# Two placeholder activations around the group norm, in a four-layer vision network

## The chip, the cores and the metric

The kernel runs on one core of one Trainium2 chip. Its time is the device time of one execution in microseconds (us), and of several runs the median counts.

## The reference

The input is four images of 56 by 56 pixels with 128 channels. Each image passes through four layers, and each layer adds its result to its input. Every layer begins with a group norm over groups of four channels:

- L0 and L3 are window transformers. Windows of 7 by 7 pixels (shifted by 3) attend within themselves with four heads; then the whole image of 3136 pixels attends to itself with four heads, after a layer norm; then comes a two-layer network with a Gelu, after another layer norm.
- L1 is a state-space layer: a projection, a 3 by 3 convolution of each channel with a Silu, a softplus for the step sizes, a scan over the image in four directions with 16 states, a layer norm, a gate and a projection back.
- L2 is a deformable convolution: offsets from a 3 by 3 convolution, a gather of four neighbours for each of nine taps, their weighted sum and a product with the kernel.

The part that matters here, as the kernel computes it: for each group of four channels, the mean and the variance over channels and pixels, then (x - mean) / sqrt(variance + 1e-5).

## The kernel before, in words

All data is kept as channels by pixels: 128 partitions, 3136 columns, worked on in 7 chunks of 448. `run` loops over the images; for each it calls `swin("L0")`, `mamba`, `deform` and `swin("L3")` on the same tile `x`. Inside each layer the order of instructions on each engine is the order in which they are written (`manual_schedule`).

- Statistics (`stats`, line 115) are taken by VectorE chunk by chunk, as soon as the layer before has stored a chunk. `group_norm` (line 117) joins them: VectorE aggregates (line 121), TensorE averages the means over each group with a matrix (line 123), VectorE makes the group variances (lines 125 to 128), TensorE averages those (line 130, tile `gn_pv`), ScalarE takes the root (line 132), VectorE the reciprocal (line 133). Three calls lead to it: in `attention` (both transformers), in `mamba_conv` and in `deform`.
- In a transformer, `windows` (line 197) returns the steps of the window attention, and the loop in `attention` writes them out interleaved: tokens (line 222, VectorE and GpSimd, the normalised pixels `xw`), project (line 230, TensorE, `pq` and `pk`), queries and keys (lines 235 and 241, ScalarE, Identity with a bias), scores (lines 257 to 264), exponentials (line 267, ScalarE, Exp), and so on. GpSimd fills several tiles with zeros at the start (lines 219, 225, 323, 324, 377). The layer norm of the image attention follows the windows and takes a root for each chunk (line 158), so that Exp and Sqrt alternate from the fourth row of windows on.
- The last step of a transformer, `mlp`, ends on ScalarE with the Gelu (line 680) and on VectorE with the store of a chunk (line 690). After L3 the chunk is written out and the next image's chunk is read into the same columns (`finish`, lines 1381 and 1383).
- `mamba_conv` starts with the normalised chunks (line 137), the projection (line 765, tile `pi`), its copies by ScalarE (line 769) and the convolution; its first function with a table of its own is Silu (line 791).
- `deform` uses only copies and Identity on ScalarE after its group norm.

ScalarE works from a table of functions that has to be loaded when the next function is not in the one at hand. No line of the kernel asks for it: the compiler puts an ACT_TABLE_LOAD ahead of the first activation that needs another table, and the profile books it under that activation's line. Copy, Identity and Square need none.

Of the kernel before, what the change touches and what calls it, by code (L numbers as in the profile page):

```python
# [10 lines left out]
F32 = mybir.dt.float32  # L11
F32R = mybir.dt.float32r
I32 = mybir.dt.int32
AF = mybir.ActivationFunctionType
# [5 lines left out]
P = 128  # L20
# [50 lines left out]
def _offsets(cols):  # L71
    at, n = {}, 0
    for name, w in cols:
        at[name] = (n, w)
        n += w
    return at, n


class _Net:
    def __init__(self, ctx, tc, x, packs, out):  # L80
        self.tc, self.nc, self.x_in, self.out = tc, tc.nc, x, out
        self.B = x.shape[0]
        nc = self.nc
        wp = ctx.enter_context(tc.tile_pool(name="weights", bufs=1))
        self.keep = wp
        self.w = {}
        for i, (layer, cols) in enumerate(COLS.items()):
            at, n = _offsets(cols)
            t = wp.tile([P, n], F32, tag=f"w_{layer}", name=f"w_{layer}")
            (nc.sync if i % 2 == 0 else nc.scalar).dma_start(t, packs[layer])  # L90
            self.w[layer] = {name: t[:, o : o + k] for name, (o, k) in at.items()}
        c = self.w["C"]
        self.ident, self.gmat = c["ident"], c["gmat"]
        self.ones = {1: c["ones1"], 2: c["ones2"]}
        self.center = {1: (c["center1"],), 2: (c["center2"], c["others2"])}
        self.sel = wp.tile([P, KB], F32R, tag="sel", name="sel")
        nc.vector.memset(self.sel.bitcast(F32), 0.0)
        for h in range(NH):
            nc.vector.memset(self.sel[h * DK : h * DK + 2, :].bitcast(F32), 1.0)
        self.ident2 = wp.tile([64 + NX, NX], F32R, tag="ident2", name="ident2")  # L100
        nc.vector.memset(self.ident2.bitcast(F32), 0.0)
        for k in (0, 64):
            nc.vector.tensor_copy(self.ident2[k : k + NX, :], self.ident[:NX, :NX])
        self.one32 = wp.tile([P, DK], F32, tag="one32", name="one32")
        nc.vector.memset(self.one32, 1.0)
        self.eps = wp.tile([P, 1], F32, tag="eps", name="eps")
        nc.vector.memset(self.eps, 1e-5)
        self.x = wp.tile([P, L], F32, tag="x", name="x")
        self.st = wp.tile([P, NCK, 6], F32, tag="gn_st", name="gn_st")
        self.dpool = ctx.enter_context(tc.tile_pool(name="tables", bufs=1, space=DRAM))  # L110


    def stats(self, x, c):

        self.nc.vector.bn_stats(self.st[:, c, :], x[:, c * CH : (c + 1) * CH])

    def group_norm(self, sb, ps):
        nc = self.nc
        st = self.st
        mv = sb.tile([P, 2], F32, tag="gn_mv", name="gn_mv")  # L120
        nc.vector.bn_aggr(mv, st.rearrange("p c s -> p (c s)"))
        pm = ps.tile([P, 512], F32, tag="mm", name="gn_pm")
        nc.tensor.matmul(pm[:, 0:1], lhsT=self.gmat, rhs=mv[:, 0:1], start=True, stop=True)
        mean = sb.tile([P, 1], F32, tag="gn_mean", name="gn_mean")
        nc.vector.tensor_copy(mean, pm[:, 0:1])
        dv = sb.tile([P, 1], F32, tag="gn_dv", name="gn_dv")
        nc.vector.tensor_sub(dv, mv[:, 0:1], mean)
        nc.vector.scalar_tensor_tensor(dv, dv, dv, mv[:, 1:2], ALU.mult, ALU.add)
        pv = ps.tile([P, 512], F32, tag="mm", name="gn_pv")
        nc.tensor.matmul(pv[:, 0:1], lhsT=self.gmat, rhs=dv, start=True, stop=True)  # L130
        rstd = sb.tile([P, 1], F32, tag="gn_rstd", name="gn_rstd")
        nc.scalar.activation(rstd, pv[:, 0:1], AF.Sqrt, bias=self.eps)
        nc.vector.reciprocal(rstd, rstd)
        return mean, rstd
# [172 lines left out]
    def attention(self, layer, x, x1, oT, sb):  # L307
# [32 lines left out]
        with tc.manual_schedule():  # L340
# [33 lines left out]
            with tc.tile_pool(name="ap_sb", bufs=2) as tb, tc.tile_pool(name="ap_ps", bufs=8, space=PSUM) as ps:  # L374
                bank = lambda name: ps.tile([P, 512], F32, tag="mm", name=name)
                of_windows = self.windows(layer, x, x1, self.group_norm(tb, ps), tb, bank)
                nc.gpsimd.memset(kl, 0.0)
                ln = {}

# [1108 lines left out]
```

## Time and profile before

| what | value |
|---|---|
| median of 3 runs | 13458.64 us (13451.59 to 13462.05) |
| profiled execution, its own time | 13245.72 us |
| its span from first to last instruction | 13243.9 us |
| mean granted TensorE clock | 0.933 |
| ScalarE busy | 7563.6 us (57%) |
| ACT_TABLE_LOADs under line 132 | 8, of 1283 ns each |
| ACT_TABLE_LOADs under line 267 | 48, of 1283 ns each |
| group norms (line 132, ACTIVATE) | 16, of 261 ns each |

By the first instruction of each group norm, one image takes some 860 us in L0, 1220 us in L1, 367 us in L2 and 862 us in L3. Engines in the profile are PE (TensorE), PEld (its weight loads), DVE (VectorE), ACT (ScalarE), POOL (GpSimd) and SP (SyncE, which issues most DMAs). A line of the timeline gives the start, the duration, the engine, the line of the kernel, the operation, its output and inputs; in brackets stands the idle time of the engine ahead of it and what ended that. A line of the stretches gives the busy time and the number of instructions of PE, PEld, DVE, ACT and POOL in order, then the granted clock, the busy share of the DMA engines and GB/s.

### The profile page before, as it was taken

The numbers are of one execution on the slowest core, as the hardware profiler recorded it, in microseconds if no ns is written. First come the engines' busy times: TensorE is split into PE (matmuls) and PEld (weight loads), VectorE is DVE, ScalarE is ACT, GpSimd is POOL, SyncE is SP. The second block draws the span as 40 slices with busy tenths as digits, with TensorE's granted clock in tenths as the row PEclk, the third lists the DMA queues.
The fourth block names the chain that finished last, engine by engine and source line by source line (L and its number), as shares of the span: only waits on it lengthen the run. The fifth ranks groups of instructions, "written<-read, shape, count | busy, mean of one in ns | idle before, by whom it ended". The sixth has DMA issues, their size and how long they took to land. (4 is left out here: it accounts for less than half of the span.)

```text
span 13243.9 us, 218251 instructions
## 1 busy us (share of the span) xinstructions
PE 11713.7 (88%) x85716; PEld 7459.5 (56%) x85716; DVE 9575.5 (72%) x11831; ACT 7563.6 (57%) x19130; POOL 9941.6 (75%) x6852
## 2 busy tenths in 40 slices
PE   8999995699898999579989899957999989995799
PEld 4448884444544888444454488834445448883444
DVE  6649996665665999666466499966646649996664
ACT  5567772356556777235655677723565567772356
POOL 4949995488494999548849499954975949995497
PEclk9999997799999999779999999977999999996799
DMA  2000004200000000420000000042000000004200
GB/s 100 1 14 4 5 4 118 78 1 6 6 1 14 4 5 4 120 75 1 8 4 1 14 5 5 4 125 70 1 9 2 1 14 5 5 4 130 65 1 6
DMA packets 181178, 344.60 MB, mean 26 GB/s; under 512 B 20104, under 2 KB 101416, under 8 KB 180024
## 3 DMA queue, kind: packets, MB, share of 16 engines
q0 software_dynamic: 80640, 231.28, 6.3%
q1 hardware_dynamic: 99224, 97.83, 2.4%
q8 instruction: 678, 11.11, 0.4%
q14 instruction: 348, 2.85, 0.1%
q10 hardware_dynamic: 288, 1.53, 0.0%
HBM read 256.04 MB, written 74.52 MB: 25 GB/s over the span
## 5 line engine op out<-in xcount | busy, mean ns | idle before, releaser
L555 POOL TENSOR_TENSOR es<-es,e 128x896 f32<-128x896 f32 x2016 | 4158.8, 2088 | 133.0 <-ACT e L549 75.0
L350 DVE TENSOR_REDUCE mx<-pm 128x1 f32<-128x512 f32 (+1 forms) x4928 | 3056.5, 670 | 1411.1 <-PE pm L349 795.8
L549 ACT ACTIVATE e<-pst 128x448 f32<-128x448 f32 (+1 forms) x5600 | 2677.6, 544 | 1893.3 <-PE pst L547 1348.1
L1066 DVE TENSOR_TENSOR_SCAN hs<-da,dbu 128x928 f32<-128x928 f32 x1792 | 3633.0, 2070 | 53.2 <-ACT dbu L1059 29.3
L1075 POOL TENSOR_TENSOR hs<-hs,cb 128x896 f32<-128x896 f32 x1792 | 3486.9, 1963 | 26.0 <-ACT carry L1070 20.8
L349 PE MATMUL pm<-ks,qs 32*128 32x512 f32 (+1 forms) x9856 | 2911.8, 636 | 13.4 <-DVE nm L371 7.8
L547 PE MATMUL pst<-qs,ks 32*128 32x448 f32 x11200 | 2685.4, 547 | 0.0
L1084 PE MATMUL yt<-w_C,hs 128*116 128x128 f32 x14336 | 1865.8, 273 | 1.1 <-POOL hs L1075 1.1
L542 PE MATMUL pst<-nm,sel 32*128 32x448 f32 x5600 | 1638.7, 614 | 0.0
L1084 PEld LDWEIGHTS yt<-w_C,hs 128*116 128x116 f32 x14336 | 1570.5, 135 | 2.1 <-POOL hs L1075 2.1
L1048 PE MATMUL dbu<-dgb,ut 112*128 112x224 f32 x7168 | 1258.5, 298 | 268.8 <-DVE hs L1066 268.7
L571 PE MATMUL po<-e,va 128*32 128x448 f32 (+1 forms) x11200 | 1352.4, 551 | 0.1
L349 PEld LDWEIGHTS pm<-ks,qs 32*128 32x128 f32 x9856 | 924.3, 186 | 745.2 <-DVE mx L350 618.9
L1325 POOL DMA_INDIRECT g<-tab,idx x1008 | 940.5, 933 | 452.9 <-issue 425.8
L1048 PEld LDWEIGHTS dbu<-dgb,ut 112*128 112x128 f32 x7168 | 945.3, 192 | 534.2 <-DVE hs L1066 524.2
L1002 ACT ACTIVATE da<-dl,A 128x112 f32<-128x112 f32 x3584 | 1194.6, 383 | 0.1
L547 PEld LDWEIGHTS pst<-qs,ks 32*128 32x128 f32 x11200 | 1098.0, 185 | 102.6 <-issue 13.7
L1351 PE MATMUL pvt<-w_C,g 112*128 112x112 f32 x2016 | 404.5, 367 | 729.3 <-issue 607.8
L542 PEld LDWEIGHTS pst<-nm,sel 32*128 32x128 f32 x5600 | 570.6, 184 | 740.2 <-DVE mx L350 387.1
L1352 ACT COPY vt<-pvt 128x336 f32<-128x336 f32 x336 | 147.2, 438 | 1188.0 <-PE pvt L1351 1184.5
L1351 PEld LDWEIGHTS pvt<-w_C,g 112*128 112x128 f32 x2016 | 315.2, 203 | 823.1 <-issue 784.2
L1070 ACT COPY carry<-hs 128x32 f32<-128x32 f32 x1792 | 397.5, 222 | 623.3 <-DVE hs L1066 615.2
(230 smaller groups left out, 15791.4 us busy)
## 6 DMA issues: line engine op xcount, KB each, us to landing
tab<-zero SPq DMA_DIRECT2D x4, 6728.0 KB
g<-tab,idx POOLq DMA_INDIRECT x1008, 3.5
tab<-gt SPq DMA_DIRECT2D x32, 448.0 KB
dl_d<-dl SPq DMA_DIRECT2D x28, 448.0 KB
dl<-dl_d SPq DMA_DIRECT2D x56, 224.0 KB
tab<-gt SPq DMA_DIRECT2D x32, 336.0 KB
out_dram<-x SPq DMA_DIRECT2D x28, 224.0 KB
x<-in_x_dram SPq DMA_DIRECT2D x21, 224.0 KB
```

The lines of the kernel that those rows point to most:

```text
L349: nc.tensor.matmul(pm[:, :m], lhsT=qs[head(h), q.start : q.start + P], rhs=ks[head(h), keys], start=True, stop=True)
L350: nc.vector.tensor_reduce(mx[:, home[i][1], h, kc : kc + 1], pm[:, :m], AX.X, ALU.max)
L542: nc.tensor.matmul(t[:, :CH], lhsT=self.sel[head(h), :], rhs=nm[head(h), part(qc)], start=True, stop=False)
L547: nc.tensor.matmul(t[:, :CH], lhsT=ks[head(h), k * KB : (k + 1) * KB], rhs=qs[head(h), part(qc)], start=False, stop=True)
L549: nc.scalar.activation(e[:nk, j, :], t[:nk, :CH], AF.Exp, scale=SCALE)
L555: nc.gpsimd.tensor_tensor(s, es[g - 1, p][:nk] if k == 1 else s, e[:nk], ALU.add)
L571: nc.tensor.matmul(m["po"][head(h), :CH], lhsT=va[:nk, k, head(h)], rhs=src(h)[:nk], start=(k == 0), stop=(k == NKB - 1))
L1002: nc.scalar.activation(m["da"][:, :, n, 2:], dl(), AF.Exp, scale=A[:, j, n : n + 1])
L1048: nc.tensor.matmul(pu[:, 8 * h : 8 * h + 8, 2 + tb * TB : 2 + (tb + 1) * TB], lhsT=made[g]["ut", 2 * r + tb][:, d, :], rhs=made["r", g // ...
L1066: nc.vector.tensor_tensor_scan(flat(pairs[u // 2][:, d % 2]), flat(made[g]["da"][:, r]), flat(banks.pop(u)), 0.0, ALU.mult, ALU.add)
L1075: nc.gpsimd.tensor_tensor(hs, hs, made["r", g // 2]["cb"][:, :, r * HW : (r + 1) * HW], ALU.mult)
L1084: nc.tensor.matmul(sums[q][:YR, e * P : (e + 1) * P], lhsT=hs[:, n, :], rhs=self.ident, start=(n == 0), stop=(n == NST // 2 - 1), is_trans ...
```

## The change

A helper `table_of(f)` writes one activation of function `f`, 128 by 1, from the constant tile `eps` into a new tile `any` that nothing reads. `group_norm` calls it with Sqrt as its first instruction, ahead of the aggregation, in all four layers. `attention` calls it with Exp straight after its group norm, ahead of the first instruction of the windows. Nothing else is moved or removed; which table is loaded where follows from the compiler.

```diff
+        self.any = wp.tile([P, 1], F32, tag="any", name="any")
...
+    def table_of(self, f):
+
+        self.nc.scalar.activation(self.any, self.eps, f)
+
     def group_norm(self, sb, ps):
         nc = self.nc
         st = self.st
+        self.table_of(AF.Sqrt)
         mv = sb.tile([P, 2], F32, tag="gn_mv", name="gn_mv")
...
                 of_windows = self.windows(layer, x, x1, self.group_norm(tb, ps), tb, bank)
+                self.table_of(AF.Exp)
                 nc.gpsimd.memset(kl, 0.0)
```

## The prediction

> **What bounds the kernel now.** I read the page's busy times first, then the stretches by stage, then ScalarE's groups by line, and last the timeline around the group norms.
>
> ```profile
> PE 11713.7 (88%) x85716; PEld 7459.5 (56%) x85716; DVE 9575.5 (72%) x11831; ACT 7563.6 (57%) x19130; POOL 9941.6 (75%) x6852
> ```
>
> ScalarE (ACT) is busy 57% of the span, so a change to it counts only where another engine stands still for it. In the stretches, TensorE is busy over 90% in every transformer and scan stage, and half busy in the four gather stages. All those stages begin with a group norm, and there nothing runs beside the chain. The groups of ScalarE by line (columns: count, busy us, mean ns, idle before) show the table loads:
>
> ```profile
> L158 ACT ACT_TABLE_LOAD x132 | 169.4, 1283 | 2.3
> L132 ACT ACT_TABLE_LOAD x8 | 10.3, 1283 | 56.2 <-PE gn_pv L130 56.2
> L267 ACT ACT_TABLE_LOAD x48 | 61.6, 1283 | 0.8
> L132 ACT ACTIVATE gn_rstd<-gn_pv,eps 128x1 f32<-128x1 f32 x16 | 4.2, 261 | 99.3 <-PE gn_pv L130 99.2
> ```
>
> There are 16 group norms (4 images by 4 layers) and 8 loads. The view of line 132 gives the wait for gn_pv in front of a load 7 times, in front of the ACTIVATE 9 times. So 7 loads begin only when the variance is there. The timeline of one of them, the second image's first layer (start us, duration):
>
> ```profile
> 3326.12 2.89 ACT L680 ACTIVATE h<-ph,w_L 128x448 f32<-128x448 f32 x4 [1.11 <-PE ph L679]
> ...
> 3338.56 1.80 POOL L225 MEMSET pz<- 128x2048 f32 x1
> ...
> 3339.81 1.28 ACT L132 ACT_TABLE_LOAD   x1 [10.80 <-PE gn_pv L130]
> 3341.10 0.26 ACT L132 ACTIVATE gn_rstd<-gn_pv,eps 128x1 f32<-128x1 f32 x1
> 3341.39 0.16 DVE L133 RECIPROCAL gn_rstd<-gn_rstd 128x1 f32<-128x1 f32 x1 [2.31 <-ACT gn_rstd L132]
> 3341.67 0.89 DVE L222 TENSOR_SCALAR xw<-x,gn_mean,gn_rstd 128x343 f32<-128x343 f32 x3
> ...
> 3344.44 0.74 ACT L235 ACTIVATE qp<-pq,w_L 128x196 f32<-128x196 f32 x2 [3.08 <-PE pq L230]
> 3345.75 2.41 ACT L241 ACTIVATE kb<-pk,w_L 32x392 f32<-32x392 f32 x4 [0.56 <-PE pk L230]
> 3348.17 1.28 ACT L267 ACT_TABLE_LOAD   x1
> ...
> 3352.43 0.86 ACT L267 ACTIVATE s<-s 128x784 f32<-128x784 f32 x1 [2.98 <-DVE s L264]
> ```
>
> ScalarE stood 10.80 us idle, then loaded, while VectorE waited 2.31 us for the root. Where the root's table still stood from the layer before, the wait is shorter:
>
> ```profile
> 2471.62 0.26 ACT L132 ACTIVATE gn_rstd<-gn_pv,eps 128x1 f32<-128x1 f32 x1 [11.19 <-PE gn_pv L130]
> 2471.92 0.16 DVE L133 RECIPROCAL gn_rstd<-gn_rstd 128x1 f32<-128x1 f32 x1 [0.82 <-ACT gn_rstd L132]
> ```
>
> **What the skill says.** "ScalarE: Activation LUTs", section "What ACT_TABLE_LOAD costs": 1283 ns for a load, and with a drain of about 1380 ns some 2.66 us for a switch. The trace has the 1283 ns in every row; it shows no drain at these seven, since ScalarE had been idle, and the ACTIVATE follows the load's end by 0.01 us. The same page, "Table sets: the hidden batching unit": root and exponential are in different sets, and copies and the like are in every set. The trace agrees: the Identity at line 235 and the Square at line 383 take no load. "TensorE: Matmul & The Clock Gate", section "What's actually happening": the clock falls to half after an idle window of about 3.4 us and rises after a busy one, and the windows run freely. The trace has the halving (below). "SBUF — State Buffer", section "Who interferes with whom": VectorE's two-port operations and GpSimd shut one another out of a shared port. The trace has such a case (third rival).
>
> **The change, part by part.** (1) The root's load leaves the chain at seven places: the first layer of images 2 to 4 and the scan layer of all four images. The eighth, at 10.03 us, already ran ahead. By durations, ACTIVATE moves from 3341.10 to 3339.81: 1.29 us. By the other route, VectorE's waits at line 133 are 2.11 to 2.31 us with a load and 0.82 to 1.03 without; like clock against like (2.11 against 0.83) gives 1.28. Seven by 1.29 is **9.0 us**. Bounds: zero, if the load is held anyway, and 7 by 2.66 = 18.6 us, the skill's switch. I take the trace's value.
>
> (2) The new Sqrt carries that load. It waits for nothing but the memset of eps at the start; in its queue it stands behind the last Gelu. Load and ACTIVATE take 1.28 + 0.26 (nearest row: the ACTIVATE of line 132) = 1.54 us, in a pause of 10.80 us in the first layer (second image). In the scan layer the last Gelu ends at 871.89 + 2.89 = 874.78 and the wait ends at 880.68, 5.90 us. Cost nothing; with the pause gone it would be the 9.0 us again plus 0.26 each. The other eight have no load or an 11 us pause; the same 0.26 hides. No DMA is issued, and no other queue changes.
>
> (3) The new Exp, eight times, stands behind the group norm's root. Its load passes the Identities of lines 235 and 241 and leaves line 267. It holds back queries(0), keys(0), and behind them the scores' PE and VectorE work, if it is late. It isn't: load and ACTIVATE need 1.54 us, and the pause until pq comes is 3.08 here (3.07 in the first image, 3.41 or more in the fourth layer). At least 1.5 us is left over. At line 267 the load ran inside the wait for the scores: 2.98 us of idle time remained after it. So its removal gains nothing. Bounds of this part: 0 and 0; without the cover it would cost 8 by 1.54 = 12.3 us.
>
> (4) What is late next. In the scan layer, VectorE's normalisation follows the reciprocal at once, and TensorE waits for it: the gain goes through. In the first layer xw would start at 3341.67 - 1.29 = 3340.38; GpSimd's last memset ends at 3338.56 + 1.80 = 3340.36, and the sums for images 3 and 4 come within 0.02 us of that too. At most some hundredths are lost. Every later stage needs these results, so no slack downstream takes it back.
>
> (5) One tile of four bytes a partition moves later tiles. No row prices an address; I take nothing, and the range's outer parts stand for it.
>
> Sum: 13245.72 (the profiled execution; its span is 13243.9) - 9.0 = 13236.7. The median of the runs, 13458.64, lies 212.9 above that execution. I don't know what fills the difference; the stretches saved are fixed durations, so I subtract the same 9.0: **13449.6**. The three runs differ by 10.5 us among themselves. About 0.2%, 26.9 us, is what a measurement of this kernel can tell from no change.
>
> **The rivals.** *Nothing lifted* (13458.6): the new load is held by a wait as line 132's was, or the load stays there. For it: line 132's load stood behind waits of its own instructions. Against: tile any is never read and never released, so there is nothing to wait for.
>
> *The clock gains too* (13438.8): in the scan layer TensorE restarts at half clock.
>
> ```profile
> 878.00:882.00 4.00, 0.74 (x4) 0.59 (x4) 1.45 (x5) 1.31 (x2) 0.95 (x4) 1.00 0.00 0
> 882.00:890.00 8.00, 6.97 (x11) 3.36 (x12) 4.05 (x15) 2.37 (x5) 0.00 (x0) 0.57 0.00 0
> 890.00:950.00 60.00, 60.00 (x154) 25.75 (x153) 49.04 (x71) 37.02 (x50) 0.00 (x0) 1.00 0.06 22
> ```
>
> The column before the last two is the granted clock: 1.00, then 0.57, then 1.00. The fall lies near 882.4, 0.6 us before the twelve pi matmuls begin; a start 1.29 us earlier comes before it. The twelve took 7.76, 7.09, 6.34 and 7.70 us in the four images; at full clock 12 by 0.376 (the spacing of the weight loads just ahead of the pause) is 4.51. At most 28.9 - 18.0 = 10.9 us more could go. Against: the windows run freely, and a later fall may slow the same matmuls; a part of 0 to 4 us is likelier.
>
> *The port is lost* (13462.1, slower): at the start of the fourth layer VectorE's xw and GpSimd's memsets meet. In image 1 the three xw took 5.63 us, in image 2 1.45: once VectorE got the port after one memset, once only after all. That is 4.2 us a time, for a matter of nanoseconds. If the three images that escaped are caught in the new run, 12.5 - 9.0 leaves +3.5. It decides from three new losses on. Against: the change doesn't touch what these two engines do there.
>
> **How the numbers follow.** Forecast 0.74, nothing lifted 0.08, clock gains 0.12, port lost 0.06. The forecast's own range is 13441 to 13458 (the scatter of the median and a few us of clock). The wide range reaches to the clock case and to the port case: 13438 to 13462. Faster than 13431.7 needs the clock's bound and luck: 0.04. Slower than 13485.6 is in none of the cases; 0.03 for addresses and the like.
>
> **What would show it.** Line 132 has no table loads; the line of the new helper has sixteen (8 Sqrt, 8 Exp), each ended well before the wait behind it ends; line 267's loads fall from 48 to 40; the waits of VectorE at the reciprocal sum to 23.5 - 9.0 = 14.5 us; ScalarE's pause ahead of queries(0) shrinks, while the distance from reciprocal to first score stays. A load behind gn_pv, or queries(0) later than pq, would prove me wrong. So would a stage in between that grew by over 5 us.

## The result and the profile after

The changed kernel took 13453.56 us (median of 12 runs, 13439.11 to 13464.33), the kernel before 13461.34 in 12 runs beside it: ratio 0.9992, 95% interval 0.9984 to 1.0. That is less than 0.2%, and since the interval reaches 1.0, no difference is sure at all. The time lies in the forecast range and 4 us from the forecast. The trace, however, shows that the forecast 9 us were not gained in the place where they were forecast.

ScalarE's groups in the changed kernel (count, busy us, mean ns, idle before; the change moves the group norm's root from line 132 to 138, the exponentials from 267 to 273, and adds line 120 for the placeholders):

```profile
L164 ACT ACT_TABLE_LOAD x132 | 169.4, 1283 | 2.4
L273 ACT ACT_TABLE_LOAD x47 | 60.3, 1283 | 0.8
L120 ACT ACT_TABLE_LOAD x16 | 20.5, 1283 | 1.9 <-PEq L1487 1.7
L138 ACT ACT_TABLE_LOAD x8 | 10.3, 1283 | 56.2 <-PE gn_pv L136 56.2
L120 ACT ACTIVATE any<-eps 128x1 f32<-128x1 f32 x24 | 4.9, 203 | 0.4
```

The row of line 138 is that of line 132 before, to the digit: 8 loads, 56.2 us of waiting for gn_pv in front of them. The placeholders did not take them over; they brought 16 loads of their own, and only one left the exponentials (47 for 48). The waits of VectorE say the same:

```profile
DVE gn_rstd L139 <- ACT gn_rstd L138: 23.5, 16, 2.3
```

That is 23.5 us in 16 waits, as before; I had forecast 14.5. The timeline of ScalarE at the first layer of the second image shows where the placeholders went:

```profile
3373.38 2.89 ACT L687 ACTIVATE h<-ph,w_L 128x448 f32<-128x448 f32 x4 [1.11 <-PE ph L686]
3387.03 1.28 ACT L138 ACT_TABLE_LOAD   x1 [10.76 <-PE gn_pv L136]
3388.32 0.26 ACT L138 ACTIVATE gn_rstd<-gn_pv,eps 128x1 f32<-128x1 f32 x1
3388.60 1.28 ACT L120 ACT_TABLE_LOAD   x1
3389.90 0.20 ACT L120 ACTIVATE any<-eps 128x1 f32<-128x1 f32 x1
3390.12 1.28 ACT L120 ACT_TABLE_LOAD   x1
3391.41 0.20 ACT L120 ACTIVATE any<-eps 128x1 f32<-128x1 f32 x1
3391.66 0.74 ACT L241 ACTIVATE qp<-pq,w_L 128x196 f32<-128x196 f32 x2
...
3395.36 0.44 ACT L120 ACTIVATE any<-eps 128x1 f32<-128x1 f32 x2
3395.82 1.28 ACT L273 ACT_TABLE_LOAD   x1
```

Between the last Gelu and the load of line 138 stands nothing: the pause of 10.76 us is empty, although the source calls the Sqrt placeholder there. Behind the root follow four placeholders. The first is Exp, where it is written. The second needs another load, so it is a Sqrt; the two at 3395.36 need none, so they are Sqrts too. By their number, the same at every first layer, they are those of the next three layers (scan, gather, fourth). The Sqrt of this very layer had then run in the image before, behind the Exp of its fourth layer, where one more Sqrt stands.

So the table changes to Exp and back to Sqrt in the pause ahead of the queries, and to Exp again at line 273. That costs nothing by luck: two loads and two activations end at 3391.61, and the queries start at 3391.66, 3.04 us behind the reciprocal, as before the change.

### The profile page after: what moved, and what is told of

It reads as the page before. It is cut to its first block, busy times and chain, and to the rows that moved or that the text cites. A ratio compares the mean times of both kernels' runs of the same rounds, so it can differ in the third digit from the quotient of the medians.

```text
span 13451.8 us, 218282 instructions
## 1 busy us (share of the span) xinstructions
PE 11676.7 (87%) x85716; PEld 7445.1 (55%) x85716; DVE 9571.8 (71%) x11831; ACT 7579.2 (56%) x19169; POOL 9941.3 (74%) x6852
```

## The experiments

All times below are set against the kernel before on the same chip, in the same comparison. That kernel itself took 13461 us in the comparison of the result, whose chip isn't on record, 13238 us on chip 6 (its repeat, the held placeholders, the first Sqrt alone, the sixteen loads), 13468 us on chip 14 (the moved addresses and the cover) and 13234 us on chip 13 (the others). So times of different comparisons are not compared.

### The kernel before again

> The kernel before once more, unchanged, for the scatter and for a second profile of it. Expected by every theory of the change: ratio 1.000 within 0.1%. It also tests where the 213 us lie that separate the profiled execution of before (13245.7) from its median: if they lie in the gather stages, as the trace of the changed kernel suggests (about 424 us from the third to the fourth group norm of each image, against 367 in the profile of before), the new profile of the old kernel shows about 424 four times and a time near 13455; if the changed kernel itself had slowed the gather, the new profile shows 367 four times.

Measured: 13237.53 against 13238.15, ratio 0.9999 (0.9991 to 1.0008). Neither expectation on the 213 us was the right one: the times went with the chip. The gather stage of the first image, in the changed kernel (first line) and in this one (second), in columns start:end, length, busy and count of PE, PEld, DVE, ACT, POOL, then clock, DMA share, GB/s:

```profile
2103.00:2526.00 423.00, 173.94 (x792) 115.83 (x792) 253.37 (x295) 40.66 (x94) 235.83 (x256) 0.63 0.54 152
```

```profile
2103.00:2468.00 365.00, 177.29 (x768) 115.90 (x760) 251.06 (x293) 40.24 (x91) 244.32 (x263) 0.62 0.63 175
```

The same work takes 58 us longer in the first, with the DMA engines less busy. Summed over four images, from reciprocal to the next group norm, the gather stages took 1684.5 against 1457.2 us, and the other three layers differ by 13. That is where the 213 us lie. It isn't the change: in the four profiles of chip 14, one of them without any placeholder, the gather stages took 1665 to 1678 us, and in the eight of chips 6 and 13, five of them with placeholders, 1452 to 1458. Why the gather differs between chips stays open.

### Held placeholders

```diff
+        self.any = wp.tile([P, NCK], F32, tag="any", name="any")
...
     def table_of(self, f):
-        self.nc.scalar.activation(self.any, self.eps, f)
+        self.nc.scalar.activation(self.any, self.st[:, :, 0], f, bias=self.eps, scale=0.0)
```

> Both placeholder activations, but they read a column of the group norm's statistics (scaled by zero, plus eps), so that none can run before the statistics of its own layer exist. Theory 1 (displaced: the changed kernel ran its Sqrt placeholders one or more layers too early, and the loads stayed on the chain): no load under the group norm's own line (0 instead of 8), VectorE's waits at the reciprocal 14.5 us instead of 23.5, time 9 us under before, ratio about 0.9993. Theory 2 (the load's time is absorbed later, wherever it is loaded): the same 14.5 us at the reciprocal, but the stages that follow grow by as much, ratio 1.000. An interval of some 0.1% cannot tell the two apart by the time alone; the distances from the reciprocal to the first matmuls and scores do.

Measured: ratio 0.9990 (0.9983 to 0.9996), 13 us under before. Two stretches of ScalarE's timeline, at the first image's scan layer and the second image's first layer:

```profile
871.93 2.89 ACT L687 ACTIVATE h<-ph,w_L 128x448 f32<-128x448 f32 x4 [1.11 <-PE ph L686]
874.84 1.28 ACT L120 ACT_TABLE_LOAD   x1
878.65 0.31 ACT L120 ACTIVATE any<-gn_st,eps 128x7 f32<-128x7 f32 x1 [2.52 <-DVE gn_st L116]
880.76 0.26 ACT L138 ACTIVATE gn_rstd<-gn_pv,eps 128x1 f32<-128x1 f32 x1 [1.81 <-PE gn_pv L136]
...
3327.93 0.26 ACT L138 ACTIVATE gn_rstd<-gn_pv,eps 128x1 f32<-128x1 f32 x1 [2.22 <-PE gn_pv L136]
3328.21 1.28 ACT L120 ACT_TABLE_LOAD   x1
3329.51 0.31 ACT L120 ACTIVATE any<-gn_st,eps 128x7 f32<-128x7 f32 x1
3331.27 0.74 ACT L241 ACTIVATE qp<-pq,w_L 128x196 f32<-128x196 f32 x2 [1.46 <-PE pq L236]
```

Now the load follows the last Gelu at once, and the root starts without one. Line 138 has no load any more, and VectorE's waits at the reciprocal are

```profile
  ACT gn_rstd L138: 14.3, 16
```

against 23.5. The way from the aggregation to the reciprocal, summed over the 16 group norms, fell from 48.6 to 39.1 us. This is the prediction's point 1, in the place and size that it gave. The Exp placeholder leaves 1.46 us of its pause; point 3 had said at least 1.5.

That these 9 us reach the end isn't shown by this profile. From the reciprocal to the next group norm its four first layers took 3416.7 us, against 3402.6 in the repeat of before, though the first exponentials there came no later (11.04 us behind the reciprocal, against 11.04 to 12.71). In the profiles of kernels whose chain is as before, the same sum lies between 3395 and 3403 us.

### Sqrt alone, twice

```diff
-                self.table_of(AF.Exp)
```

> The change with the Sqrt placeholder alone, without the Exp one. Theory 1: with no placeholder of another kind between them and nothing to wait for, all 16 Sqrt placeholders are placed at the very start of the kernel, ahead of the first group norm; the group norms keep 7 loads on the chain; no load is added in the transformers' pauses; VectorE's waits at the reciprocal stay at 23.5 us; ratio 1.000. If the placeholders were only displaced because they queue behind the Exp ones, each would now stand in its own layer, with no load on the chain and 14.5 us.

Measured: the placement as expected, the time not. The start of the kernel on ScalarE:

```profile
1.67 1.28 ACT L120 ACT_TABLE_LOAD   x1 [1.67 <-PEq L1486]
2.96 0.20 ACT L120 ACTIVATE any<-eps 128x1 f32<-128x1 f32 x1
...
9.99 1.28 ACT L120 ACT_TABLE_LOAD   x1
11.29 3.48 ACT L120 ACTIVATE any<-eps 128x1 f32<-128x1 f32 x15
22.25 0.26 ACT L138 ACTIVATE gn_rstd<-gn_pv,eps 128x1 f32<-128x1 f32 x1 [7.48 <-PE gn_pv L136]
```

All sixteen Sqrts, for four images and four layers, have run by 14.8 us. Seven loads remain behind gn_pv, and the reciprocal's waits are 23.5 us:

```profile
L138 ACT ACT_TABLE_LOAD x7 | 9.0, 1283 | 56.2 <-PE gn_pv L136 56.2
```

Yet the ratio was 0.9988 (0.9981 to 0.9995), 11 us under before, with nothing on the chain changed. The held version, beside it on chip 6, had a median of 13225.19 us against 13226.68 here: 1.5 us apart, where the waits at the reciprocal differ by 9.2 us. The same kernel again:

> The kernel with the Sqrt placeholder alone, once more. Its first measurement was 11 us under before although nothing on the chain differs, and a moved tile alone gained nothing. If those 11 us were a draw (how the four starts of the fourth layer share the port between VectorE and GpSimd, and where the clock's windows fall), they are not found again: ratio 1.000 with an interval that holds 1. If they are a property of the program, about 0.9988 again.

Measured: 0.9993 (0.9985 to 1.0001), again some 10 us under, but with 1 inside the interval. This bears out neither expectation cleanly.

### Sixteen loads more on the chain

```diff
+        for i in range(8):
+            nc.scalar.activation(rstd, pv[:, 0:1], AF.Exp, bias=self.eps)
+            nc.scalar.activation(rstd, pv[:, 0:1], AF.Sqrt, bias=self.eps)
         nc.scalar.activation(rstd, pv[:, 0:1], AF.Sqrt, bias=self.eps)
```

> The kernel before, with eight pairs of Exp and Sqrt activations of the same input ahead of each group norm's root: 247 loads more and 256 activations more, all behind the variance and ahead of the reciprocal. If the time of a load on this chain goes through to the end (theory 1 and the prediction's point 4): 247 x 1.28 + 256 x 0.26 = about 383 us more, 13845, ratio about 1.028. If later stages absorb part of it (theory 2): clearly under 1.02. More than 1.030 would mean that the longer pauses cost something of their own, the clock of TensorE first.

Measured: ratio 1.0277 (1.026 to 1.0295), 372 us more. VectorE's waits at the reciprocal, 416.7 us against 23.5:

```profile
  ACT gn_rstd L135: 416.7, 16
```

So 393 us were added to the chain and 372 reached the end, 95%. Time added to the chain goes through; theory 2 falls for an addition of this size. Against the profile of the kernel before on this chip, the fourth layers were 13.7 us shorter from the reciprocal on. Some 2 us of that are the first queries, 3.04 to 3.05 us behind the reciprocal instead of 3.42 to 3.62: with the group norm later, GpSimd's memsets are over before VectorE starts, and the first three xw take 0.89 us in each instead of 1.25 to 1.46. The rest isn't accounted for.

### The moved addresses

```diff
         nc.vector.memset(self.eps, 1e-5)
+        space = wp.tile([P, 1], F32, tag="space", name="space")
+        nc.vector.memset(space, 0.0)
```

> The kernel before with nothing but one more tile of four bytes a partition, written once and never read, at the place where the change puts its tile: every later tile moves up by 32 bytes, and no activation and no load changes. Sqrt alone gained 11 us although its loads stayed on the chain and its instructions differ from before in three rows at the very start. If the moved addresses made that gain (theory A), this kernel has it too: ratio about 0.999, 9 to 13 us under before. If they did not (theory B: something in the placeholder activations, or only the draw of the clock's windows), the ratio is 1.000.

Measured: 1.0003 (0.9994 to 1.0011). On this chip the address isn't the cause; theory A falls. Theory B, an effect of the placeholders away from the chain or a draw, stays. Two more runs keep every tile in its place, the change and the held version, with the placeholder's result in the eps tile. The held version's edit is shown; for the change, `any` is column 1 alone:

```diff
-        self.eps = wp.tile([P, 1], F32, tag="eps", name="eps")
-        nc.vector.memset(self.eps, 1e-5)
+        eps = wp.tile([P, 8], F32, tag="eps", name="eps")
+        nc.vector.memset(eps, 1e-5)
+        self.eps, self.any = eps[:, 0:1], eps[:, 1:8]
```

> The change as it is, but its result goes into the unused part of the eps tile, so that no other tile moves. The activations and the loads stand where the change has them. Theory A: ratio 1.000, since nothing of the load's part reaches the end. Theory B: about 0.999, as the change itself. In both the reciprocal's waits stay at 23.5 us.

Measured: 0.9998 (0.9989 to 1.0006), 2.8 us under before, waits 23.9 us.

> The held placeholders, again without moving a tile. Reciprocal's waits 14.4 us. Theory A, with the load's time going through to the end: 9 us under before, ratio 0.9993, and the held kernel with moved tiles should then be faster than this one. Theory A with the load's time absorbed later: ratio 1.000. Theory B: 13 us under before, 0.999.

Measured: 0.9987 (0.998 to 0.9993), 17.9 us under before, waits 14.8 us. With nothing moved, the change shows no gain, while the held version lies 15 us under the change, which ran beside it. The 9 us of the chain fit into that; the other 6 have no place in the trace. On chip 6 the two kernels that differ in the same way, held and Sqrt alone, lay 1.5 us apart, so one comparison of this kind doesn't settle what the 9 us are worth.

### The cover taken away

```diff
-                self.table_of(AF.Exp)
+                for i in range(9):
+                    self.table_of(AF.Sqrt if i % 2 else AF.Exp)
```

> The held placeholders, with nine activations in place of the one Exp after the transformer's group norm, Exp and Sqrt by turns, so that ScalarE switches its table nine times in the pause ahead of the first queries: 9 x (1.28 + 0.27) = 14.0 us in pauses of 3.1 us (first layer) and 7.8, 3.6, 3.6 and 3.4 us (fourth layer). If the cover is as the prediction says, the first queries come 10.9 us late in the first layer and 6 to 10.6 us in the fourth: 4 x 10.9 + 6.2 + 3 x 10.4 = 81 us more than the held kernel, ratio to before about 1.005. If the later windows absorb a late start: no slower than 0.999.

Measured: 1.0036 (1.0022 to 1.0049), 48 us over before. Against the held version with unmoved tiles, which ran beside it on the same chip, it is 66 us more. ScalarE at the second image's first layer, its first and last placeholders:

```profile
3397.00 0.26 ACT L138 ACTIVATE gn_rstd<-gn_pv,eps 128x1 f32<-128x1 f32 x1 [2.22 <-PE gn_pv L136]
3397.28 1.28 ACT L120 ACT_TABLE_LOAD   x1
3398.57 0.31 ACT L120 ACTIVATE any<-gn_st,eps 128x7 f32<-128x7 f32 x1
...
3410.22 1.28 ACT L120 ACT_TABLE_LOAD   x1
3411.52 0.30 ACT L120 ACTIVATE any<-gn_st,eps 128x7 f32<-128x7 f32 x1
3411.73 0.72 ACT L241 ACTIVATE qp<-pq,w_L 128x196 f32<-128x196 f32 x2
```

A switch takes 1.61 us here, a little over my 1.55. The first queries start 14.44 us behind the reciprocal at all eight places: 11.1 to 11.4 us later than in the held version in the first layers, and 6.6 to 6.9 us later in the fourth, where they had started at 7.5 to 7.8. That makes 72 us (my 81 had counted three short pauses), of which 66 reached the end. The pause is a real limit: two switches, as the change makes them, fit with 0.05 us to spare. By these figures, an estimate, a third would have come about 1.5 us too late.

### Exp alone, no root, and a start without GpSimd's port

```diff
-        self.table_of(AF.Sqrt)
```

> The change with the Exp placeholder alone. By every theory the Exp load moves from the line of the exponentials into the pause ahead of the first queries, and nothing on the chain changes: reciprocal's waits 23.5 us, 8 loads under the group norm's line, 40 under the exponentials, first queries after the group norm no later than before (3.04 us in the first layer), ratio 1.000. Slower than 1.001 would show that the Exp load costs something in the pause.

Measured: the places as expected (8 loads at the group norm, 8 at the placeholder, 40 at the exponentials, waits 23.6 us, queries after 3.04 to 3.05 us), and a ratio of 0.9989 (0.9981 to 0.9998), 10 us under before, for which no step of the chain gives a reason. The next kernel leaves the group norm's root out, so that nothing has to be loaded there:

```diff
-        nc.scalar.activation(rstd, pv[:, 0:1], AF.Sqrt, bias=self.eps)
+        nc.scalar.activation(rstd, pv[:, 0:1], AF.Identity, bias=self.eps)
```

> The kernel before with Identity in place of the group norm's root (so it leaves the root out, and divides by the variance): no table for the root is loaded in the group norm, no placeholder is added and no tile is moved. It is the most that the change could have brought. Expected if a load's time on the chain goes through: 9 us under before, 0.9993, with the reciprocal's waits at 14.5 us. If it is absorbed: 1.000. If less work on ScalarE has an effect of its own: 0.998 or under.

Measured: waits 14.4 us, ratio 0.9990 (0.9984 to 0.9997), 12 us under before. Its ratio is that of the held version. Beside it on chip 13, the two kernels with all loads on the chain, Sqrt alone and Exp alone, are only 2.0 us slower.

The last kernel is the held version with unmoved tiles, without the Exp placeholder and with the first windows normalised by ScalarE:

```diff
-                self.table_of(AF.Exp)
...
+            if t == 0:
+                nb = sb.tile([P, 1], F32, tag="gn_nb", name="gn_nb")
+                nc.vector.scalar_tensor_tensor(nb, gn[0], -1.0, gn[1], ALU.mult, ALU.mult)
             for (a, r, c), at in self.window_pieces(order[t]):
+                if t == 0:
+                    nc.scalar.activation(xv[:, a, r, c], self.piece(img, at), AF.Identity, bias=nb, scale=gn[1])
...
```

> The held Sqrt placeholder without the Exp one, and the first normalised windows made by ScalarE (Identity with scale and bias, 3 instructions, one small VectorE operation more for the bias) in place of VectorE, so that GpSimd's memsets cannot keep them waiting. First queries after the reciprocal: about 3.3 us at all eight starts, against 3.04 in the first layer and 3.4 to 7.8 in the fourth. Where all four starts of the fourth layer were caught (7.6 to 7.8), that saves 4 x 4.4 - 4 x 0.3 = 16 us beyond the held kernel, ratio to before about 0.9975; where none was, nothing, 0.999. If the starts of the windows do not set the end of the stage, nothing either way.

Measured: first queries 3.62 to 3.64 us behind the reciprocal at all eight starts, ratio 0.9989 (0.9982 to 0.9997). In the other profiles of this chip most fourth-layer starts were not caught by GpSimd's memsets (3.4 to 3.6 us; one of twelve took 7.8), so there was little to save. On a chip where all are caught it wasn't tried.

## Why the prediction was right, and where it was wrong

The time was right and the way to it wrong. What came true in the trace is the first rival, nothing lifted, which I had given 0.08: the load stayed where it was, for a cause that I hadn't written. That the median still fell within 4 us of the forecast was luck. The forecast range ends 0.6 us below that rival's 13458.6, and an interval of 0.0016, over 21 us wide, can't tell 9 us from nothing.

- **The step that failed is (2)**: "in its queue it stands behind the last Gelu". The Sqrt placeholder did not stand there but in earlier layers, up to an image too early; so all 8 loads stayed under the group norm's line, 7 of them on the chain, and the waits stayed at 23.5 us. The placements fit one rule, which no run shows directly: the order of the source holds inside one layer's block, and an instruction that comes first on its engine there and reads nothing made there can move ahead into earlier blocks, up to the placeholder before it, which writes the same tile. The placeholder read only a constant and wrote a tile that nobody reads. I took that as the reason that it could never be late, and overlooked that it could then also be early. Sqrt alone shows it purely (15 of 16 in one row at 11.29 us), and the held version is the reverse: one true input, and it stays.
- **Point 1**, seven loads of 1.29 us on the chain, is borne out at the reciprocal by the held version and by the kernel without the root: 23.5 to 14.3 and 14.4 us of waiting. What that is worth at the end stays open.
- **Point 3** is borne out for the Exp placeholder: it stayed in its place, behind the root on which its block depends, and cost nothing. But the pause held one Sqrt switch more than I had counted, and was full. So the forecast sixteen loads under the helper's line, 8 for Sqrt and 8 for Exp, came true by chance, with the Sqrts in the wrong places.
- **Point 4**, that nothing downstream takes the chain's time back, holds for delays: 372 of 393 us and 66 of 72 us came through. For the 9 us taken away it isn't shown: beside kernels with placeholders and all loads on the chain, the shorter chain was 1.5 us faster on chip 6, 2.0 us on chip 13 and 15 us on chip 14.
- **Point 5** held on the chip where it was tried: moved addresses gave 1.0003.
- **The second rival**, the clock, shows no such gain. In the versions with the shorter chain, the twelve pi matmuls took 26.9 to 28.9 us over four images, in those with the chain as before 27.5 to 30.9; at full clock, as the prediction worked it out, they would take 18.0.
- **The third rival's mechanism is real**, though it is no effect of the change. In the four profiles of chip 14, all 16 starts of a fourth layer were caught; in the profile of the changed kernel none was. One of each, GpSimd's memset of pz and the three xw behind the reciprocal, first the unmoved change, then the change. In the first the xw end behind the last memset, 2528.97 + 1.82 = 2530.79; in the second they start beside the first memset of pz and are done soon after it:

```profile
2525.97 5.43 DVE L228 TENSOR_SCALAR xw<-x,gn_mean,gn_rstd 128x343 f32<-128x343 f32 x3
2528.97 1.82 POOL L231 MEMSET pz<- 128x2048 f32 x1
```

```profile
2528.22 1.81 POOL L231 MEMSET pz<- 128x2048 f32 x1
2529.26 1.45 DVE L228 TENSOR_SCALAR xw<-x,gn_mean,gn_rstd 128x343 f32<-128x343 f32 x3
```

What stays open is the 8 us between the medians of the result, whose interval reaches 1.0. Kernels with the chain as it was came out at 0.9988, 0.9989, 0.9992 (the change), 0.9993, 0.9998, 0.9999 and 1.0003; those with the chain shortened at 0.9987, 0.9989, 0.9990 and 0.9990. The second group is lower on the average, by about 0.0006, which is near the 9 us. But the first group spreads by 0.0015 without any cause on the chain, so single programs seem to differ by some 10 us for reasons that I haven't settled. One rival is untested: in the first group the two kernels without a placeholder came out at 0.9999 and 1.0003, the five with one at 0.9992 on the average. A placeholder may have an effect away from the chain, though the kernel without the root has none of them and came out at 0.9990. Two differences that the traces do show between single executions are the caught starts, 4 us each, and TensorE's clock: from 787 to 800 us behind the reciprocal in the first layer of the first image, the profile of before and its repeat have

```profile
809.60:822.60 13.00, 12.45 (x32) 6.86 (x32) 1.48 (x3) 8.87 (x12) 1.13 (x1) 0.57 0.00 0
```

```profile
809.50:822.50 13.00, 13.00 (x55) 7.77 (x54) 3.20 (x7) 10.98 (x16) 1.13 (x1) 1.00 0.00 0
```

with a clock of 0.57 and of 1.00, and this layer took 856.1 and 848.0 us. By an estimate from these figures, 13.00 x 0.43, at most 5.6 of the 8.1 us are the clock's in this stretch. Neither was tried by itself.

Of the versions run, the held one (0.9990, and 0.9987 with unmoved tiles) came out under the kernel before with an interval below 1 both times, but so did Sqrt alone (0.9988, first time) and Exp alone (0.9989), with every load still on the chain. Against the change itself it was measured with unmoved tiles only, on chip 14: 13449.99 against 13465.03 us.

## What to carry to other kernels

A placeholder that is to stand at a point of the program needs an input that exists only from that point on. Without one it can be put earlier, as here, and its effect is undone by the next switch. Check such a change by the rows it should empty (here, the loads under the group norm's line), not by the total. A total in the range is no proof of the steps: two errors of 9 us, or one and a draw of the same size, don't show in 13,450.

## What the runs showed of the hardware that I had not expected

- The same kernel took 13468 us on chip 14 and 13234 and 13238 us on chips 13 and 6; in the profiles compared, the gather stage of the first image took 423 against 365 us.
- Load and activation of 128 by 7 in a row of nine table switches took 1.61 us a switch (1.28 the load, 0.31 the activation).
- An activation of 128 by 1 without a bias operand took 203 ns; the group norm's root, with one and with its input in the memory that TensorE writes, took 261.
- Whether VectorE gets past GpSimd's memsets at the start of a fourth layer differed between chips: 16 of 16 starts were caught on chip 14, 1 of 12 on chip 6 (without the sixteen loads) and 1 of 12 on chip 13 (without the last kernel).
